# A second FFN in seven block products for two tiles, with row statistics taken in the attention

## The chip, the cores and the metric

The kernel runs on one core of a Trainium2 chip. Its time is device microseconds from one launch to its end. Five engines work beside each other, and each takes its own instructions in a fixed order: TensorE (PE in the profile; its weight loads are PEld), VectorE (DVE), ScalarE (ACT), GpSimd (POOL) and SyncE (SP). PE writes into PSUM banks, and DVE or ACT bring the results to SBUF. Semaphores tie the engines together.

## The reference

The input x has 2048 rows (tokens) of 1024 float32 numbers. The block is a macaron: half an FFN, an attention with a convolution, half an FFN.

```python
x = x + 0.5 * ffn(layernorm(x))
x = x + attn(layernorm(x))        # convolution of width 3, then causal attention in blocks of 128 tokens
x = x + 0.5 * ffn(layernorm(x))

def ffn(x):                       # the same weights in both
    routing = softmax(x @ gate_w.T)              # 8 experts
    in_scale = routing @ in_channel_scale
    out_scale = routing @ out_channel_scale
    return x * in_scale @ sign(weight).T * out_scale + bias
```

The change is in the second FFN and in the attention ahead of it.

## The kernel before

The first FFN runs to about 200 us, the convolution to about 420, the attention to about 780, and the second FFN to the end. The rows are worked on in 16 tiles of 128.

**The second FFN (class `Ffn`).** For one tile `sums_of` takes the row statistics (two `bn_stats`, their sum, an epsilon on DVE; a power and a shift on POOL) and ACT writes the normalized rows `xn`. `transpose` turns them on PE in two halves, and ACT copies the halves into `xnT`. `gate` multiplies with the gate's weights, `route` makes the softmax over 8 experts: the largest logit on DVE (`nm`), the exp on ACT, then the reciprocal and a high and a low part (`rhl`) on DVE. `turn` transposes these on PE (`rt`) and DVE copies them (`rT`). `scale` multiplies `rT` with the input scales on PE (`is`), DVE multiplies `xnT` by them, ACT casts each half to the fp32r format (the high term), and POOL subtracts for the low term, so that two passes of matmuls keep the accuracy. `out_scale` makes the output scales on PE (`po`), and ACT halves them into `os`. `main` runs 32 matmuls of 128x512: 8 chunks of the inner dimension, 2 terms, 2 halves of the columns. DVE multiplies each half by `os` and adds it into the row. `add_bias` adds half the bias to the row by a transfer that accumulates, issued from POOL. The signs of the weights stay in SBUF (`sw2`).

**What sets the order.** `run` writes out PE's order by hand: `main` of one tile, with the gate, route, transposes and turn of later tiles between its halves. On DVE, ACT and POOL a scheduler decides the order when the kernel is built, from the program's order and its own costs. Loads and stores go through SP's queue. The row buffers of the second FFN form a ring of nine (`load_rows2`): two shared with the sign loads (`aside`), three of their own, four of the attention's ring.

**The attention.** It runs over 4 groups g of 512 tokens, and for each group 4 turns r of two pairs of heads: queries and keys (`stage_qk`), scores, softmax, transposes, values and the output weights (`stage_wo`). In the second turn of the next group `stage_proj` projects the four tiles of a group and DVE adds them to the residual rows (L1116); SP stores them. In the same turn the signs of two chunks of the FFN's weights are loaded and taken on ACT. The last group's projection lies at the end, interleaved by hand with the start of the second FFN (tiles 0 to 2).

Of the kernel before, what the change touches and what calls it, by code (L numbers as in the profile page):

```python
# [17 lines left out]
P = 128  # L18
# [6 lines left out]
def kernel(  # L25
# [42 lines left out]
    const.tile([P, 80], F32, name="left_edge")  # L68
    sbq = const.tile([P, NHP], F32, name="sbq")
    spill = pool(ctx, "spill", 1, space=DRAM)  # L70
# [117 lines left out]
    class Ffn:  # L188
# [12 lines left out]

        def norm(self, t, pinned=False, on_vector=False):
            for n in range(t, min(t + 2, self.end)):
                self.ahead(n)
            self.norm_sums(t, pinned, on_vector)()
# [8 lines left out]
        def transpose(self, t, copies=(nc.scalar.copy, nc.scalar.copy)):  # L214
            xn = self.xns.pop(t)
            xnT = self.work.tile([P, DC, P], F32, name=f"xnT_{self.name}_{t}", tag="xnT", bufs=3)
            for h, copy in enumerate(copies):
                tr = bank("tr", [P, 4, P], f"tr_{self.name}_{t}_{h}")
                for c in range(4):
                    nc.tensor.transpose(tr[:, c, :], xn[:, ts(4 * h + c, P)], ident)  # L220
                copy(xnT[:, 4 * h : 4 * h + 4, :], tr)  # L221
            self.xnTs[t] = xnT
# [66 lines left out]
        def out_scale(self, t):  # L289
            rT = self.rTs.pop(t)  # L290
            osc = self.work.tile([P, D], F32, name=f"os_{self.name}_{t}", tag="osc")
            pos = [bank("acc", [P, NB], f"po_{self.name}_{t}_{h}") for h in range(NH2)]
            for h, po in enumerate(pos):
                rows = ts(NH2 + h, QC)
                nc.tensor.matmul(po, lhsT=rT[rows, :], rhs=tables[rows, :], start=True, stop=True)
            for h, po in enumerate(pos):
                nc.scalar.mul(osc[:, ts(h, NB)], po, 0.5)  # L297
            self.oscs[t] = osc
# [48 lines left out]
        def run(self, first):  # L347

            self.behind = first > self.first
            for t in range(first, self.end):
                if t + 2 not in self.lgps:
                    self.on(self.gate, t + 2)
                if t + 1 < self.end:
                    self.scale(t + 1, out=True)
                self.main(t, 0)
                self.on(self.route, t + 2)
                self.on(self.transpose, t + 3)
                self.on(self.between, t - 2)  # L360
                self.on(self.norm, t + 4, t < self.kept)
                self.on(self.add_bias, t + 4)
                self.main(t, 1, beside={DC - 2: lambda: self.on(self.turn, t + 2)})
                self.on(self.after, t - 1)
                self.beside(t)

# [571 lines left out]
    def leave(t, h):  # L938

        if t + 1 == NT:  # L940
            nc.sync.dma_start(out=out[ts(t, P), ts(h, NB)], in_=rows[t][:, ts(h, NB)])

    with ExitStack() as ph:
        ow = pool(ph, "ow", 1)
        ap4 = pool(ph, "ap4", 4)
        vhp = pool(ph, "vhp", 1)
        ap2 = pool(ph, "ap2", 2)
        qkt.append(pool(b2, "qkt1", 1, side="right"))
# [153 lines left out]

        def stage_proj(g, b, kinds=("mm", "tr")):
# [13 lines left out]
            t = g * BPG + b  # L1117
            x3[t] = spill.tile([P, D], F32, name=f"x3_{t}")
# [16 lines left out]

        def turn(g, r, values):
# [7 lines left out]
            if r == 1:  # L1144
                raws = [signs(2 * g + n) for n in range(2)]
# [20 lines left out]
        with tc.manual_schedule(engines={mybir.EngineType.PE}):  # L1166
            for i in range(LAST - 1):
                turn(*divmod(i, NP), True)
                if i == LAST - 3:
                    for t in range(2):  # L1170
                        load_rows2(t)
                if i == LAST - 2:
                    load_residual(NG - 1)
            g, r = pairs[-1]
            begun = {}
            xn_of = {}
            for t in range(2):
                with tc.issue_after(stored[g - 1].ins):
                    begun[t] = sums_of(
                        lambda t=t: xn_of[t], rows[t], f"f2_{t}", on_vector=t, later=True  # L1180
                    )
# [4 lines left out]
            work = pool(f2, "work2", 2, side="right")  # L1186
            xn2 = pool(f2, "xn2", 3, side="right")
            later.append(pool(f2, "rring2", 3, side="right"))
            ffn = Ffn("f2", sw2, work, xn2, 0, NT, lambda t: rows[t], load_rows2, store, lambda t: None, lambda t: None, NT, leave)
            two(stage_wo, LAST - 3)  # L1190
            two(stage_transpose, LAST - 2, "sm", "tr")
            for t in range(2):
                ffn.xns[t] = xn_of[t] = xn2.tile([P, D], F32, name=f"xn_f2_{t}", tag="xn")
                begun[t]()

            def begin_tile(t):
                ffn.norm(t, t > 0)
                ffn.add_bias(t)

# [12 lines left out]
            stage_transpose(g, NHP - 1, "mm")  # L1212
            stage_wo(g, NHP - 2)
# [4 lines left out]
            with tc.issue_after(ended[g].ins):  # L1218
                begin_tile(2)
            one = ("mm", "mm")  # L1220
            stage_proj(g, 0, one)
            ffn.turn(0)
            ffn.transpose(2)
            stage_proj(g, 1, one)
            ffn.scale(0, out=True)
            ffn.route(1)
            stage_proj(g, 2, one)
            stage_proj(g, 3, one)
            ffn.turn(1)
            begin_tile(3)  # L1230
    ffn.run(0)
# [55 lines left out]
```

## Time and profile before

| | |
|---|---|
| time, median of 3 runs | 940.31 us (939.81 to 940.38) |
| the profiled execution | 940.06 us, its span 938.3 us |
| busy: PE, PEld | 920.0 us (98%), 659.5 us (70%) |
| busy: DVE, ACT, POOL | 662.3 us (71%), 462.0 us (49%), 235.7 us (25%) |
| HBM traffic | 89.30 MB read, 37.85 MB written |
| bias into a row (POOL's queue) | 5.3 us from issue to landing |
| row load, row store (SP's queue) | 4.5 us, 2.6 us |

The span is the time from the first to the last instruction that the profiler recorded. Busy is the time in which an engine had an instruction at work; matmuls are pipelined and their ends are modelled, so the sum of the lengths of single matmuls is more than the busy time. In lines of the timeline, `x2` stands for two instructions in a row, and a bracket at the end tells how long the engine had been idle and what ended that.

### The profile page before, as it was taken

The page shows a single profiled execution, that of the slowest core. Times are in us where ns is not written, and L with a number is a line of the kernel's source. Part 1 is how long each engine was busy: PE and PEld are TensorE (multiplying, and loading weights), DVE is VectorE, ACT ScalarE, POOL GpSimd, SP SyncE. Part 2 cuts the span into 40 slices and gives each one's busy share as a digit, 9 for nine tenths or more (in the row PEclk, how much of TensorE's full clock was granted, in tenths as well). Part 3 has the DMA queues.
Part 4 walks back from the last instruction along what each step waited for, and adds up shares of the span by engine and source line. Part 5 has one row for each costly group of instructions (what it writes and reads, how often), then busy time and mean ns, then how long its engine had stood idle before and what let it go on. Part 6 is the DMA issues. An engine that isn't in the chain of part 4 may idle for free.

```text
span 938.3 us, 14525 instructions
## 1 busy us (share of the span) xinstructions
PE 920.0 (98%) x5240; PEld 659.5 (70%) x5240; DVE 662.3 (71%) x1326; ACT 462.0 (49%) x1258; POOL 235.7 (25%) x330
## 2 busy tenths in 40 slices
PE   6999999999999999999999999999999999999998
PEld 4678878886666666675876577567765756788786
DVE  5888887789978677656686557656746666666654
ACT  5676666431111111126886567666855844454441
POOL 2554453220011100101231113013201404444341
PEclk9999999999999999999999999999999999999999
DMA  9776653499567765536360245032406737655341
GB/s 343 181 199 192 178 182 136 186 274 353 181 201 195 190 188 135 117 108 222 116 135 23 75 154 133 23 140 89 88 1 209 150 114 210 172 163 152 90 114 67
DMA packets 39543, 144.86 MB, mean 154 GB/s; under 512 B 5096, under 2 KB 6120, under 8 KB 37552
## 3 DMA queue, kind: packets, MB, share of 16 engines
q1 hardware_dynamic: 28048, 97.91, 28.9%
q0 software_dynamic: 10688, 38.02, 20.9%
q10 hardware_dynamic: 736, 8.02, 2.3%
q8 instruction: 41, 0.67, 0.3%
q14 instruction: 30, 0.25, 0.1%
HBM read 89.30 MB, written 37.85 MB: 136 GB/s over the span
## 4 chain that ended last, share of the span: by engine, by line
PE 80%; DVE 7%; ACT 6%; DMA 3%; issue 3%; POOL 1%; POOLq 0%; DVEq 0%; ACTq 0%
PE cv L544 23%; PE pm_f L311 19%; PE pq L829 7%; PE pp L1108 6%; PE pv L829 5%; PE acc L1084 4%; PE sc L1012 3%; PE tr_f L220 3%; PE pt L1054 2%; DMA x<-in_x_dram 2%; ACT p L1039 2%; PE ao L1067 2%; PE lgp_f L228 2%; PE is_f L272 1%; ACT qk L972 1%
## 5 line engine op out<-in xcount | busy, mean ns | idle before, releaser
L311 PE MATMUL pm_f<-sw,y_f 128*128 128x512 f32 x1024 | 258.4, 403 | 0.6 <-ACT y_f L285 0.4
L311 PEld LDWEIGHTS pm_f<-sw,y_f 128*128 128x128 f32 x1024 | 186.8, 190 | 41.9 <-ACT y_f L285 0.8
L544 PE MATMUL cv<-v,u 128*128 128x342 f32 x576 | 166.0, 450 | 0.0
L544 PEld LDWEIGHTS cv<-v,u 128*128 128x128 f32 x576 | 109.2, 190 | 56.7
L1025 POOL TENSOR_SCALAR_AFFINE_SELECT p<-p 128x512 f32<-128x512 f32 x64 | 38.5, 635 | 249.6 <-ACT p L1021 249.6
L1039 ACT ACTIVATE p<-p,anm 128x128 f32<-128x128 f32 x256 | 99.8, 396 | 0.0
L561 ACT ACTIVATE m<-cv 128x342 f32<-128x342 f32 x42 | 19.2, 456 | 154.4 <-PE cv L544 152.3
L323 DVE TENSOR_TENSOR pm_f<-pm_f,os_f 128x512 f32<-128x512 f32 x64 | 44.6, 697 | 68.6 <-PE pm_f L311 68.5
L286 POOL TENSOR_TENSOR y_f<-xnT_f,y_f 128x512 fp32r<-128x512 f32 x63 | 80.0, 1288 | 45.3 <-ACT y_f L285 45.3
L1035 DVE TENSOR_REDUCE anm<-p 128x4 f32<-128x512 f32 x64 | 39.6, 678 | 26.9 <-POOL p L1025 26.9
L1084 PE MATMUL acc<-oT,wo_sb 128*128 128x512 f32 x128 | 58.0, 595 | 0.2 <-DVE oT L1076 0.2
L544 PE MATMUL cv<-v,g 128*128 128x342 f32 (+2 forms) x224 | 57.1, 415 | 0.8 <-DVE v L466 0.8
L1108 PE MATMUL pp<-pw_sb,o2T 128*128 128x512 f32 x128 | 56.4, 596 | 0.0
L221 ACT COPY xnT_f<-tr_f 128x512 f32<-128x512 f32 x58 | 33.6, 588 | 41.6 <-PE tr_f L220 39.9
L544 PEld LDWEIGHTS cv<-v,g 128*128 128x128 f32 x224 | 39.7, 190 | 17.6 <-DVE v L466 1.2
L1039 ACT ACTIVATION_READ_ACCUMULATOR p<-p,anm 128x1 f32 x256 | 49.9, 195 | 0.0
L1059 DVE COPY pT<-pt 128x512 f32<-128x512 f32 x32 | 22.1, 690 | 38.8 <-PE pt L1054 38.8
L972 ACT ACTIVATE qk<-pq,sbq 128x256 f32<-128x256 f32 x64 | 30.0, 469 | 39.5 <-PE pq L829 39.5
L1047 DVE TENSOR_TENSOR p<-p,asum 128x512 f32<-128x512 f32 x64 | 45.1, 704 | 1.3
L1108 PEld LDWEIGHTS pp<-pw_sb,o2T 128*128 128x128 f32 x128 | 23.7, 190 | 29.1 <-issue 26.1
L297 ACT ACTIVATE os_f<-po_f 128x512 f32<-128x512 f32 x64 | 34.8, 595 | 16.8 <-PE is_f L272 6.7
L285 ACT CAST y_f<-xnT_f 128x512 fp32r<-128x512 f32 x64 | 37.6, 626 | 11.1 <-DVE xnT_f L283 11.1
(186 smaller groups left out, 1668.0 us busy)
## 6 DMA issues: line engine op xcount, KB each, us to landing
g<-in_conv_w_dram SPq DMA_DIRECT2D x28, 512.0 KB, 5.2
u<-in_conv_w_dram POOLq DMA_DIRECT2D x24, 512.0 KB, 6.1
x<-in_x_dram SPq DMA_DIRECT2D x16, 512.0 KB, 5.5
raw<-in_weight_t_dram SPq DMA_DIRECT2D x16, 512.0 KB, 6.5
x<-hbias POOLq DMA_DIRECT2D x16, 512.0 KB, 5.3
x<-x SPq DMA_DIRECT2D x16, 512.0 KB, 4.1
xr<-x SPq DMA_DIRECT2D x16, 512.0 KB, 4.9
xr<-in_proj_b_dram POOLq DMA_DIRECT2D x16, 512.0 KB, 9.1
```

Source lines behind the costliest of these rows:

```text
L286: lows[h].tensor_tensor(yl, y, yh.bitcast(F32), ALU.subtract)
L311: ins = nc.tensor.matmul(pms[h], lhsT=y[:, n, c, :], rhs=self.sw[:, c, ts(h, NB)], start=(c == 0 and n == 0), stop=(c == DC - 1 and n == 1),)
L323: nc.vector.tensor_tensor(pms[h], pms[h], o, ALU.mult)
L544: nc.tensor.matmul(accs[w, k][:, lo:hi], lhsT=uk[:, c, :], rhs=V[k][:, c, lo:hi], start=(c == 0), stop=(c == DC - 1),)
L829: nc.tensor.matmul(leave.sums[sums], lhsT=rows[a][:, u, :], rhs=cols[b], start=n in (0, 1, 3), stop=True, skip_group_check=True,)
L972: nc.scalar.activation(h, acc, AF.Identity, bias=bias, scale=(QSCALE, 1.0)[n])
L1025: nc.gpsimd.affine_select(out=p, in_=p, pattern=[[0, BPG], [-1, P]], compare_op=ALU.is_ge, fill=NEG_INF, base=0, channel_multiplier=1,)
L1035: nc.vector.tensor_reduce(nmax, p, AX.X, ALU.max, negate=True)
L1039: exps[g, r] = nc.scalar.activation(p[:, b, :], p[:, b, :], AF.Exp, bias=nmax[:, b : b + 1], accum_out=asum[:, b : b + 1],)
L1047: nc.vector.tensor_tensor(p, p, asum.unsqueeze(2).broadcast_to([P, BPG, P]), ALU.mult)
L1084: nc.tensor.matmul(accs[g][m], lhsT=wo_sb[:, hp, ts(m, P)], rhs=oT, start=(hp == 0), stop=(hp == NHP - 1),)
L1108: nc.tensor.matmul(pp, lhsT=o2T[:, m, ts(b, P)], rhs=pw_sb[:, m, ts(h, NB)], start=(m == 0), stop=(m == WC - 1),)
```

## The change

The second FFN takes two tiles at a time. With the tiles as rows and halves of the inner dimension as columns, a pair's scaled input is four blocks a11, a12, a21, a22, the signs are four blocks b11 to b22, and the output is four blocks. A form of Strassen's and Winograd's multiplication makes the output from seven products (the class's `PRODUCTS`) in place of eight. It needs four sums of input blocks (s1 to s4, on DVE; s1 takes the place of a21), four sums of sign blocks (t1 to t4), and sums of products, which partly accumulate in PSUM and partly are added on DVE from copies that ACT makes. The new class `Pairs` writes out the order of a pair (`period`).

- The low terms of all seven blocks are made on DVE, not on POOL.
- The row statistics of tiles 0 to 11 are taken in the attention, in `stage_proj`, as soon as their rows are complete, and kept in small tiles. Tiles 12 to 15 keep theirs in the second FFN.
- The output goes to a tile of its own (`to`), and a transfer that accumulates, on POOL's queue, adds it to the row, for tiles 0 to 13. The last pair is added on DVE and stored by halves.
- The signs are loaded 2, 3 and 3 chunks in the first three groups, where it was 2 in each of the four, and the 16 sums of sign blocks are made on DVE in the last turns of the attention and beside the last projection.
- At the start, tiles 0 to 3 are normalized, transposed and gated, and tiles 0 and 1 scaled, before the first main product.
- There are more buffers: `xnT` has four, the high and low terms eight of half size, the output scales four.

```diff
     sbq = const.tile([P, NHP], F32, name="sbq")
+    means, rstds, shifts = (
+        [const.tile([P, BPG, n], F32, name=f"{name}_{g}") for g in range(NG - 1)]
+        for name, n in (("means", 2), ("rstds", 1), ("shifts", 1))
+    )
     spill = pool(ctx, "spill", 1, space=DRAM)
...
-        def out_scale(self, t):
+        def out_scale(self, t, kind="acc", pl=None):
             rT = self.rTs.pop(t)
-            osc = self.work.tile([P, D], F32, name=f"os_{self.name}_{t}", tag="osc")
-            pos = [bank("acc", [P, NB], f"po_{self.name}_{t}_{h}") for h in range(NH2)]
+            osc = (pl or self.work).tile([P, D], F32, name=f"os_{self.name}_{t}", tag="osc")
...
+    class Pairs(Ffn):
+        depth = 4
+        PRODUCTS = (("a11", "b11"), ("a12", "b21"), ("s2", "t2"), ("s1", "t1"), ("s3", "t3"), ("s4", "b22"), ("a22", "t4"))
...
+        def scale_in(self, t, kind):
+            xnT, rT = self.xnTs[t], self.rTs[t]
+            scs = [bank(kind, [P, 4, P], f"is_{self.name}_{t}_{h}") for h in range(NH2)]
...
+            for h, sc in enumerate(scs):
+                y = xnT[:, 4 * h : 4 * h + 4, :]
+                nc.vector.tensor_tensor(y, y, sc, ALU.mult)
+        def block_sums(self, p):
+            (a11, a12), (a21, a22) = (
+                [self.xnTs[t][:, 4 * h : 4 * h + 4, :] for h in range(2)] for t in (2 * p, 2 * p + 1)
+            )
+            s2, s3, s4 = (self.sp.tile([P, 4, P], F32, name=f"{n}_{p}", tag=n) for n in ("s2", "s3", "s4"))
+            sub = nc.vector.tensor_tensor
+            sub(s3, a11, a21, ALU.subtract)
+            sub(a21, a21, a22, ALU.add)
+            sub(s2, a21, a11, ALU.subtract)
+            sub(s4, a12, s2, ALU.subtract)
+            self.blocks[p] = {"a11": a11, "a12": a12, "s1": a21, "a22": a22, "s2": s2, "s3": s3, "s4": s4}
+        def split(self, p, *names):
+            for n in names:
+                a = self.blocks[p][n]
+                y = self.halves[p, n] = self.yp.tile([P, 2, 4, P], F32R, name=f"y_{self.name}_{p}_{n}", tag="y")
+                nc.scalar.copy(y[:, 0], a)
+                nc.vector.tensor_tensor(y[:, 1], a, y[:, 0].bitcast(F32), ALU.subtract)
+            if "a22" in names:
+                for t in (2 * p, 2 * p + 1):
+                    del self.xnTs[t]
+        def product(self, p, n):
...
+            acc = self.sums_of_pair[p][(0, 1, 0, 1, 0, 1, 0)[n]]
+            a, b = self.PRODUCTS[n]
+            y = self.halves.pop((p, a))
+            for c in range(4):
+                for part in range(2):
+                    nc.tensor.matmul(
+                        acc,
+                        lhsT=y[:, part, c, :],
+                        rhs=self.cols[b][c],
+                        start=(n in (0, 1, 3) and c == 0 and part == 0),
+                        stop=(c == 3 and part == 1),
+                        skip_group_check=True,
+                    )
+            i, h, first, last = {
+                0: (0, 0, True, False),
+                1: (0, 0, False, True),
+                2: (0, 1, True, False),
+                3: (1, 1, True, False),
+                4: (1, 1, False, True),
+                5: (0, 1, False, True),
+                6: (1, 0, True, True),
+            }[n]
+            t = 2 * p + i
+            if t not in self.outs:
+                self.outs[t] = self.tp.tile([P, D], F32, name=f"to_{t}", tag="to")
+            o, osc = self.outs[t][:, ts(h, NB)], self.oscs[t][:, ts(h, NB)] if last else None
+            if first and last:
+                nc.vector.tensor_tensor(o, acc, osc, ALU.mult)
+            elif first:
+                nc.scalar.copy(o, acc)
+            else:
+                nc.vector.tensor_tensor(o, acc, o, ALU.add)
+                nc.vector.tensor_tensor(o, o, osc, ALU.mult)
+            if not last:
+                return
+            if t + 2 >= self.end:
+                xt = self.row(t)[:, ts(h, NB)]
+                nc.vector.tensor_tensor(xt, xt, o, ALU.add)
+                self.leave(t, h)
+            elif n > 4:
+                nc.gpsimd.dma_start(out=self.row(t), in_=self.outs[t], accum_op=ALU.add)
+                self.store(t)
+        def period(self, p):
+            c, d, e, f, g, h = (2 * p + k for k in range(2, 8))
+            more = d < self.end
+            self.product(p, 0)
+            for t in (g, h):
+                self.on(self.ahead, t)
+            for t in (c, d):
+                self.on(self.turn, t)
+            self.product(p, 1)
+            if more:
+                self.scale_in(c, "tr")
+                self.scale_in(d, "acc")
+                self.block_sums(p + 1)
+                self.split(p + 1, "a11", "a12")
+            self.product(p, 2)
+            self.on(self.transpose, e)
+            if more:
+                self.split(p + 1, "s2", "s1")
+            self.product(p, 3)
+            self.on(self.transpose, f)
+            self.on(self.begin_tile, g)
+            if more:
+                self.split(p + 1, "s3")
+            self.product(p, 4)
+            for t in (e, f):
+                self.on(self.gate, t)
+            if more:
+                self.out_scale(c, "acc", self.op)
+                self.out_scale(d, "tr", self.op)
+                self.split(p + 1, "s4")
+            self.product(p, 5)
+            for t in (e, f):
+                self.on(self.route, t)
+            self.on(self.begin_tile, h)
+            if more:
+                self.split(p + 1, "a22")
+            self.product(p, 6)
...
+        def row_statistics(g, b):
+            mv, rs = means[g][:, b, :], rstds[g][:, b, :]
+            stats = small.tile([P, NH2, 6], F32, name=f"st_f2_{g}_{b}", tag="stats")
+            for h in range(NH2):
+                nc.vector.bn_stats(out=stats[:, h, :], in_=rows[g * BPG + b][:, ts(h, NB)])
+            nc.vector.bn_aggr(out=mv, in_=stats)
+            nc.vector.tensor_scalar(rs, mv[:, 1:2], EPS, None, ALU.add)
+            nc.gpsimd.tensor_tensor(rs, rs, nhalf, ALU.pow)
+            nc.gpsimd.tensor_scalar(shifts[g][:, b, :], mv[:, 0:1], rs, -1.0, ALU.mult, ALU.mult)
         def stage_proj(g, b, kinds=("mm", "tr")):
...
             t = g * BPG + b
+            if g + 1 < NG:
+                row_statistics(g, b)
...
+        SIGNS = (range(2), range(2, 5), range(5, 8), ())
...
-                raws = [signs(2 * g + n) for n in range(2)]
+                raws = [signs(c) for c in SIGNS[g]]
...
+                if i == LAST - 4:
+                    first = [
+                        vt.tile([P, WC, HE], F32R, name="t3", tag="wv_sb"),
+                        vt.tile([P, 3, NB], F32R, name="t2", tag="wv_sums"),
+                        vt.tile([P, 3, HT], F32R, name="t2_last", tag="vs"),
+                        vt.tile([P, WC, NB], F32R, name="t4", tag="vx"),
+                    ]
+                    b11, b12, b21, b22 = (
+                        [sw2[:, 4 * j + c, ts(h, NB)] for c in range(4)] for j in range(2) for h in range(NH2)
+                    )
+                    t3 = [first[0][:, c // 2, ts(c % 2, NB)] for c in range(4)]
+                    t2 = [first[1][:, c, :] for c in range(3)] + [first[2].rearrange("p n e -> p (n e)")[:, 0:NB]]
+                    t4 = [first[3][:, c, :] for c in range(2)]
+                    cols = {"b11": b11, "b21": b21, "t2": t2, "t1": b12, "t3": t3, "b22": b22, "t4": t4}
+                    def sign_sums(*names):
...
+                            for o, x0, x1 in zip(out_, in0, in1):
+                                nc.vector.tensor_tensor(o, x0.bitcast(F32), x1.bitcast(F32), ALU.subtract)
                 if i == LAST - 3:
+                    sign_sums("t3", "t1")
                     for t in range(2):
                         load_rows2(t)
                 if i == LAST - 2:
+                    sign_sums("t2")
                     load_residual(NG - 1)
             g, r = pairs[-1]
-            begun = {}
-            xn_of = {}
-            for t in range(2):
-                with tc.issue_after(stored[g - 1].ins):
-                    begun[t] = sums_of(
-                        lambda t=t: xn_of[t], rows[t], f"f2_{t}", on_vector=t, later=True
-                    )
             stage_qk(g, r)
...
+            def normalize2(t):
+                load_rows2(t)
+                g, b = divmod(t, BPG)
+                if g + 1 == NG:
+                    ffn.norm_sums(t)()
+                    return
+                xn = ffn.xns[t] = xn2.tile([P, D], F32, name=f"xn_f2_{t}", tag="xn")
+                if t == 1:
+                    nc.vector.tensor_scalar(xn, rows[t], means[g][:, b, 0:1], rstds[g][:, b, :], ALU.subtract, ALU.mult)
+                else:
+                    nc.scalar.activation(xn, rows[t], AF.Identity, bias=shifts[g][:, b, :], scale=rstds[g][:, b, :])
+            def begin_tile(t):
+                normalize2(t)
+                ffn.add_bias(t)
+            ffn.begin_tile = begin_tile
...
             stage_values(g, NHP - 2)
             stage_transpose(g, NHP - 1, "mm")
+            begin_tile(2)
             stage_wo(g, NHP - 2)
             stage_values(g, NHP - 1)
             ffn.route(0)
             ffn.gate(1, "tr")
             stage_wo(g, NHP - 1)
             with tc.issue_after(ended[g].ins):
-                begin_tile(2)
+                begin_tile(3)
+            inner.close()
+            ys = pool(f2, "ys", 8, side="right")
+            sp = pool(f2, "sp", 1, side="right")
+            tp = pool(f2, "tp", 3, side="right")
+            ffn.begin(cols, store, ys, sp, tp)
             one = ("mm", "mm")
+            ffn.transpose(2)
             stage_proj(g, 0, one)
             ffn.turn(0)
-            ffn.transpose(2)
+            ffn.route(1)
             stage_proj(g, 1, one)
-            ffn.scale(0, out=True)
-            ffn.route(1)
+            ffn.scale_in(0, "tr")
+            ffn.turn(1)
+            ffn.transpose(3)
+            sign_sums("t4")
             stage_proj(g, 2, one)
+            ffn.scale_in(1, "acc")
+            ffn.block_sums(0)
+            ffn.gate(2)
+            ffn.gate(3)
+            ffn.split(0, "a11", "a12", "s2")
             stage_proj(g, 3, one)
-            ffn.turn(1)
-            begin_tile(3)
-    ffn.run(0)
+            ffn.split(0, "s1", "s3", "s4", "a22")
+            ffn.route(2)
+            ffn.route(3)
+    with tc.manual_schedule(engines={mybir.EngineType.PE}):
+        ffn.op = pool(f2, "osc2", 4, side="right")
+        ffn.out_scale(0, "acc", ffn.op)
+        ffn.out_scale(1, "tr", ffn.op)
+        ffn.begin_tile(4)
+        ffn.begin_tile(5)
+        for p in range(NT // 2):
+            ffn.period(p)
```

## The prediction

> **What bounds the kernel now.** I read the page's totals first, then the second FFN by windows of one pair of tiles, its chain in order of time, and its timeline.
>
> ```profile
> PE 920.0 (98%) x5240; PEld 659.5 (70%) x5240; DVE 662.3 (71%) x1326; ACT 462.0 (49%) x1258; POOL 235.7 (25%) x330
> ...
> PEclk9999999999999999999999999999999999999999
> ...
> PE 80%; DVE 7%; ACT 6%; DMA 3%; issue 3%; POOL 1%; POOLq 0%; DVEq 0%; ACTq 0%
> ```
>
> TensorE is busy 98% of the span at a full granted clock. The window below is one pair of tiles (columns: window, its length, then busy time of PE, PEld, DVE, ACT, POOL, the clock, the DMA share, GB/s).
>
> ```profile
> 801.88:821.64 19.76, 19.76 (x140) 15.88 (x139) 13.07 (x31) 9.48 (x21) 8.50 (x10) 1.00 0.56 161
> ```
>
> PE fills the pair's 19.76 us and DVE uses 13.07. The chain in order of time says the same: a tile is PE work laid end to end, 9.88 us, with no other engine in it.
>
> ```profile
> 811.76 3.86 PE pm_f L311 x16
> 815.62 0.12 PE lg_f L241 x2
> 815.74 0.93 PE tr_f L220 x8
> 816.67 2.77 PE pm_f L311 x12
> 819.44 0.11 PE rt_f L260
> 819.55 0.93 PE pm_f L311 x4
> ```
>
> So fewer matmuls pay only while the other engines keep up. Their paces stand in the timeline (start, us, engine, line).
>
> ```profile
> 811.97 1.28 DVE L283 TENSOR_TENSOR xnT_f<-xnT_f,is_f 128x512 f32<-128x512 f32 x2
> 812.05 1.09 ACT L297 ACTIVATE os_f<-po_f 128x512 f32<-128x512 f32 x2
> ...
> 815.66 0.70 DVE L323 TENSOR_TENSOR pm_f<-pm_f,os_f 128x512 f32<-128x512 f32 x1 [2.41 <-PE pm_f L311]
> ...
> 816.39 0.69 DVE L324 TENSOR_TENSOR xf<-xf,pm_f 128x512 f32<-128x512 f32 x1
> ...
> 816.80 0.27 ACT L246 ACTIVATE ro_f<-lg_f,nm_f 128x8 f32<-128x8 f32 x1
> ...
> 817.20 0.16 DVE L248 RECIPROCAL rsum_f<-rsum_f 128x1 f32<-128x1 f32 x1
> ```
>
> Two independent DVE operations take 1.28, each 0.68 long, so the second starts 0.60 after the first. The add L324 needs the product L323 and starts 0.73 after it. ACT's L297 pair gives 0.49 a step, and the casts L285 (1.15 for two) 0.52. Exp to reciprocal, ACT to DVE, is 0.40. The tail shows the hand-overs and PE alone:
>
> ```profile
> 919.80 1.28 DVE L283 TENSOR_TENSOR xnT_f<-xnT_f,is_f 128x512 f32<-128x512 f32 x2
> ...
> 920.57 1.17 ACT L285 CAST y_f<-xnT_f 128x512 fp32r<-128x512 f32 x2 [0.23 <-DVE xnT_f L283]
> 921.27 2.55 POOL L286 TENSOR_TENSOR y_f<-xnT_f,y_f 128x512 fp32r<-128x512 f32 x2 [6.40 <-ACT y_f L285]
> ...
> 930.23 0.70 DVE L323 TENSOR_TENSOR pm_f<-pm_f,os_f 128x512 f32<-128x512 f32 x1 [2.28 <-PE pm_f L311]
> ...
> 933.86 0.70 DVE L323 TENSOR_TENSOR pm_f<-pm_f,os_f 128x512 f32<-128x512 f32 x1 [2.21 <-PE pm_f L311]
> ```
>
> DVE to the cast that needs it: 0.77. Cast to the low term: 0.70. Sixteen matmuls: 933.86 - 930.23 = 3.63, so 0.228 each and 1.83 for a product of eight. From the last matmul's end to DVE: 0.31 (sixteen from 811.69 end at 815.35, L323 starts at 815.66).
>
> **The change, part by part.** PE: 64 main matmuls a pair become 56: 8 x 0.228 = 1.82 less. The other PE work stays: 1.08 + 0.11 + 0.80 + 0.59 = 2.58 a tile from the chain (logits and transposes, rt, gate, scales). PE alone would need 56 x 0.228 + 5.16 = 17.9 a pair, 14.6 less over eight pairs.
>
> DVE: a pair had 12 operations of 128x512 (4 input scalings, 4 products, 4 adds) and 4 row statistics. It now has 4 scalings, 4 block sums, 7 low terms, 3 adds and 4 products: 22 x 0.60 plus dependences and some 2.5 of small routing work, nearly 16 of the period. That alone would fit into 17.9. What decides is the order: an engine takes its instructions in turn, and the built order of the changed kernel, read engine by engine, closes a loop from product 1 (a12) of one pair to product 1 of the next.
> - Product 1 runs 1.83, then 0.31: the add of products 0 and 1 starts 2.14 after it.
> - On DVE behind that add: product with the out scale 0.73, scaling 0.60, scaling 0.60; low term of a11, which waits for ACT's cast of a11 (0.77 + 0.70 after its scaling), 0.84; two scalings, s3, low a12 and s1, five steps of 0.60; s1 to s2 0.73; s2 to its cast 0.77. Sum 7.27.
> - ACT then runs without a gap: casts s2, s1 (1.04), copy of product 3 (0.49), two transpose copies (0.97), casts s3, s4 (1.04), logits copy (0.14 to the next, 811.91 to 812.05), one norm (1.15), logits copy (0.14), four out scales (1.96), cast a22 (0.52), and only then the first exp. Sum 7.45.
> - Exp to reciprocal 0.40. Then DVE: 0.16, max of the other tile 0.13, routing 0.25, low a22 0.60, routing 0.25, reciprocal 0.16, product with the out scale of product 6 0.60, routing 0.29, and 0.36 to the transpose rt. Sum 2.80.
> - rt 0.14, and PE may begin the next product 1.
>
> 2.14 + 7.27 + 7.45 + 0.40 + 2.80 + 0.14 = 20.2 a pair, against 19.76 before and 17.9 of PE's own. PE waits some 2.3 in each pair (at the second rt, and at the second gate, for ACT's copies) where it waited for nothing. The matmul saving is spent waiting on the loop.
>
> Between the starts of product 1 I take 20.2 three times. Tiles 12 to 15 still get their statistics on DVE (two of 0.60 to 0.68 a tile, some ahead of s2): 21.5 and 20.9. Then 19.9, where no norm is left on ACT but the cast of a22 waits for product 5. The next interval has no transposes and gates: 16.6, with PE's own 14.0 (12.8 of products, 2 x 0.59 of scales) as its lower bound. From the last product 1 to PE's end 6 x 1.83 = 11.0.
>
> The start: main matmuls began at 780.75. Now the transposes, gates and scalings of tiles 1 to 3 come first, and product 0 begins at about 785.4; then rt of tile 3 waits, because the exps of tiles 2 and 3 stand on ACT behind five casts and four out scales: product 1 at about 790.4. PE's end: 790.4 + 60.6 + 21.5 + 20.9 + 19.9 + 16.6 + 11.0 = 940.9. Before, it was 918.95 + 14.6 = 933.6. That is +7.3. The tail (4.7 from there to the span's end) keeps its product, add and half-row store. The three dependent steps before it (2.06) exceed the product (1.83): +0.2.
>
> Attention: the statistics of tiles 0 to 11 put 1.2 + 0.4 on DVE for each tile, 6.4 per group, into the projection stage, where DVE idles 1.02 before each of the L1116 adds; POOL's pow and shift (0.56 + 0.26) lie in front of selects (L1025) that wait for ACT anyway. Sixteen sign sums of 0.60 lie before the copies pT and queue in front of the qk adds for 0.2 to 0.35. The third sign load of a group waits for a row of the ring, with ACT idle. In the last group 3.3 of statistics go away. Together 0 to +3; I take +0.5, as the rows with idle DVE are the nearest.
>
> The residual: 14 accumulating transfers go to POOL's queue, and each store on SP waits for one. Nearest row: the bias transfer, 0.9 to issue and 5.3 to landing; with store 2.6 and next load 4.5 it is 13.3, while a row of the ring has about 30 between the end of its pair and its next use: hidden, 0. If that cover failed, the norm would be late by the excess, pair by pair. It takes three DVE adds a pair away, already counted.
>
> The low terms free POOL (four of 1.28 a pair) and load DVE with seven of 0.60, also counted; two of them lie in the loop.
>
> Sum: the profiled execution took 940.06, a span of 938.3 and 1.76 around it, 0.25 under the median. Span 938.3 + 7.3 + 0.2 + 0.5 = 946.3; with 1.76, 948.1. Forecast **948**.
>
> A rule that speaks against the change is weighed here. The row says 0.60 from one DVE start to the next. The Trainium skill, "VectorE: DVE Perf Modes", section "The DRAIN you can't avoid", says that the next operation does not start until the pipeline is empty. By it each of the loop's nine independent DVE steps would take its full 0.68, the loop 20.9 and the time about 952; the row shows a start before that, so 0.60 stands in the sum.
>
> **The rivals.** *PE stays the bound (faster).* The loop may be shorter than I add up, if ACT gets to the exps earlier or hand-overs overlap. For it: DVE, ACT and POOL each have idle time in every pair, and the chain before names only PE. Against it: the order is fixed. With the loop at or under 17.9: 790.4 + 6 x 17.9 + 14.0 + 11.0 = 922.8 instead of 933.6, plus 0.7 and 1.76 on the span, makes 930. It takes 2.3 less of waiting in each pair; at 18.9 (8.0 over six intervals) the two kernels are equal.
>
> *DVE steps at full price (slower still).* Many of the new steps wait on another engine, and the row of a step that waits is 0.73 (L323 to L324), not 0.60. Nine steps at 0.13 more make the loop 21.4, six intervals 7.0 more: 955.
>
> *A row comes late from the ring.* If accumulating, storing and loading took 30 instead of 13.3, each norm would be late: a microsecond over is six in all, so two over make 960. The DMA share of 0.56 in the window speaks against it.
>
> *The change does not do what it says.* The built order has 448 main matmuls for 512, the statistics in the attention and no low term of this FFN on POOL; excluded.
>
> **How the numbers follow.** Forecast (944 to 952 as its own range) 0.57; PE stays the bound, 928 to 937, 0.20; full price, 952 to 959, 0.15; the ring or a dearer attention 0.06; equal, 0.02. A measurement of this kernel tells 0.2%, 1.9 us, from no change. Faster 0.21, same 0.03, slower 0.76. The range leaves out the lower part of the PE rival and the ring: 934 to 958.
>
> **What would show it.** In the changed profile: PE's share below 98% in the second FFN, with waits of rt on DVE's routing and of the gate on ACT's copies; about 20.2 between products 1; DVE idle some 1.6 before the first add of a pair; exp behind four out scales on ACT; the first main matmul near 785; the attention within a microsecond. Windows of 18 with PE full would make the forecast wrong, and so would an SP store or a norm that waits for a transfer.

## The result, and the profile after

| | before | after |
|---|---|---|
| time, median | 940.35 us (939.81 to 940.86, 4 runs) | 953.74 us (953.54 to 955.66, 4 runs) |
| span of the profiled execution | 938.3 us | 951.6 us |
| first main matmul of the second FFN | 780.75 us | 787.05 us |
| its last main matmul's end | 933.6 us | 946.6 us |

The ratio is 1.0147, with an interval of 1.013 to 1.0165: the change costs 13.4 us, where 7.7 were forecast. The time lies in the wide range of the prediction (934 to 958) and above the forecast's own range of 944 to 952.

The page of the kernel after, the same three rows as before:

```profile
PE 919.1 (97%) x5176; PEld 653.5 (69%) x5176; DVE 715.4 (75%) x1426; ACT 487.9 (51%) x1306; POOL 209.8 (22%) x313
...
PEclk9999999999999999999999999999999999998999
...
PE 69%; DVE 11%; ACT 9%; DMA 6%; issue 3%; POOL 1%; POOLq 0%; DVEq 0%; ACTq 0%
```

TensorE does 64 matmuls less (5176 for 5240), but it is busy for only 0.9 us less (part of that time at half its clock, see pair 3 below), and its share of the chain falls from 80% to 69%: VectorE, ScalarE and transfers stand there now. The clock has a dent near the end.

Little of it arises before the second FFN, and none where the change adds work to the attention. The projection of group 0 begins 1.52 us later than before (528.70 for 527.18) and that of group 2 1.45 later (705.90 for 704.45), so nothing is lost between them, with the statistics and sign loads in place. Of the 1.5, 0.66 is there when the convolution begins, and the rest arises at 425 to 435 us, in the attention's first softmax, where the change moves nothing by its text.

The last row of the table is the start of the last product (944.72) and eight matmuls of 0.228. From product 1 of a pair to that of the next, by the starts in PE's timeline (the last by the middle of sixteen matmuls in a row), in us:

| pair | 0 | 1 | 2 | 3 | 4 | 5 | 6 |
|---|---|---|---|---|---|---|---|
| forecast | 20.2 | 20.2 | 20.2 | 21.5 | 20.9 | 19.9 | 16.6 |
| measured | 19.72 | 19.78 | 21.69 | 25.55 | 21.44 | 19.22 | 16.4 |

**A pair without late rows.** The chain in order of time of the kernel after (start, us, what), in pair 1; the lines left out are of the same kind:

```profile
811.74 1.84 PE pm_f L439 x8
...
813.68 0.70 DVE to L465
814.38 0.02 issue
814.40 0.69 DVE to L466
...
820.11 0.70 DVE s L415
...
824.64 1.15 ACT xn_f L1385
825.78 0.15 ACT lgs_f L242
825.93 1.96 ACT os_f L303 x4
827.89 0.51 ACT y_f_a L423
828.40 0.27 ACT ro_f L252 x2
...
830.80 0.29 DVE rhl_f L259
831.09 0.14 issue
831.23 0.30 PE rt_f L266
```

This is the loop of the prediction, in its order: product, add, scalings and block sums on VectorE, casts and copies, norm and four out scales on ScalarE, the exp (L252), the routing, the transpose. From product 1 to the add it is 2.18 (2.14 had been taken), to the cast of s2 at 820.84 7.16 (7.27), to the exp 7.56 (7.45), and from there to rt 2.83 (0.40 + 2.80). The window of that pair:

```profile
811.50:831.28 19.78, 19.00 (x131) 14.55 (x132) 15.68 (x32) 12.60 (x27) 3.44 (x5) 1.00 0.83 213
```

PE is busy 19.00 of 19.78 us. It lacks only 0.8, not the 2.3 of the forecast, because its own work is not 17.9.

**Pair 3, which the prediction had not seen.** The chain again, from the end of pair 2:

```profile
852.58 6.18 DMA xf<-to
858.76 0.02 issue
858.77 2.92 DMA out_dram<-xf
861.70 0.02 issue
861.71 6.57 DMA xf<-x
868.28 0.02 issue
868.30 0.07 DVE st_f L171
```

An accumulating transfer adds the output of tile 5 to its row, the store follows, then the load of tile 14 into the same buffer, then VectorE's statistics of that tile: 15.7 us in a row. Tile 13 takes tile 4's buffer in the same way, from 850.76 on. The timeline shows what stands behind it:

```profile
864.24 0.69 DVE L171 BATCH_NORM_STATS2 st_f<-xf 128x6 f32<-128x512 f32 x1 [2.71 <-DMA xf<-x]
864.85 0.68 DVE L415 TENSOR_TENSOR s<-xnT_f,xnT_f 128x512 f32<-128x512 f32 x1
...
867.72 0.97 PE L234 MATMUL lgp_f<-xnT_f,gate_sb 128*32 128x128 f32 x16 [3.60 <-ACT xnT_f L227]
...
869.77 3.78 PE L439 MATMUL pm_f<-sw,y_f_s 128*128 128x512 f32 x8
```

VectorE stands 2.71 us for the row of tile 13, and s2 (L415) is behind it in its order. In pair 2 it had stood 2.44 us in the same way for the row of tile 12, at 843.76. ScalarE's casts and copies come late, the gate waits 3.60, and then a product takes 3.78 us instead of 2.1. The windows around it give the granted clock in the third column from the end:

```profile
865.00:869.00 4.00, 1.22 (x18) 0.70 (x20) 3.74 (x9) 3.44 (x7) 0.00 (x0) 0.93 0.68 170
869.00:873.00 4.00, 4.00 (x12) 2.67 (x11) 3.42 (x8) 2.43 (x6) 2.19 (x3) 0.50 0.01 4
```

After the idle window TensorE ran at half its clock; that product took some 1.7 us more, and one at 892 us, in pair 4, some 1.6 more (3.66). Little of this is added to the pair, by an estimate from the timeline: the norm of tile 13, late by its statistics, runs on ScalarE at 870.93, and with the out scales behind it the exp comes only at 874.65. In pair 1 the next product 1 followed 2.88 after the exp, here 3.87 (878.52), so a full clock would have given back at most 1.0 here and, by the same count, 0.3 in pair 4. The Trainium skill, "TensorE: Matmul & The Clock Gate", section "What's actually happening", puts the drop to half rate after an idle window of about 3.4 us; the wait of 3.60 fits, while the longest single wait ahead of the second drop was 0.98.

### The profile page after: what moved, and what is told of

It reads as the page before. It is cut to its first block, busy times and chain, and to the rows that moved or that the text cites. A ratio compares the mean times of both kernels' runs of the same rounds, so it can differ in the third digit from the quotient of the medians.

```text
span 951.6 us, 14534 instructions
## 1 busy us (share of the span) xinstructions
PE 919.1 (97%) x5176; PEld 653.5 (69%) x5176; DVE 715.4 (75%) x1426; ACT 487.9 (51%) x1306; POOL 209.8 (22%) x313
## 4 chain that ended last, share of the span: by engine, by line
PE 69%; DVE 11%; ACT 9%; DMA 6%; issue 3%; POOL 1%; POOLq 0%; DVEq 0%; ACTq 0%
PE cv L692 23%; PE pm_f L317 8%; PE pq L977 8%; PE pp L1265 5%; PE pv L977 5%; PE acc L1231 4%; PE sc L1159 3%; PE pm_f L439 3%; PE pt L1201 3%; PE ao L1214 2%; DMA x<-in_x_dram 2%; ACT p L1186 2%; PE tr_f L226 2%; DVE xnT_f L405 1%; DMA xf<-to 1%
## 5 line engine op out<-in xcount | busy, mean ns | idle before, releaser
L317 PE MATMUL pm_f<-sw,y_f 128*128 128x512 f32 x512 | 132.6, 409 | 0.6 <-ACT y_f L291 0.4
L317 PEld LDWEIGHTS pm_f<-sw,y_f 128*128 128x128 f32 x512 | 94.5, 193 | 22.0 <-ACT y_f L291 0.8
L709 ACT ACTIVATE m<-cv 128x342 f32<-128x342 f32 x42 | 19.2, 456 | 153.5 <-PE cv L692 151.4
L292 POOL TENSOR_TENSOR y_f<-xnT_f,y_f 128x512 fp32r<-128x512 f32 x31 | 39.4, 1282 | 20.2 <-ACT y_f L291 20.2
L680 DVE SCALAR_TENSOR_TENSOR u<-g,u 128x1024 f32<-128x1024 f32 x18 | 22.0, 1225 | 27.7 <-issue 11.0
L1168 ACT COPY p<-sc 128x512 f32<-128x512 f32 x64 | 32.9, 600 | 16.0 <-PE sc L1159 16.0
L1231 PEld LDWEIGHTS acc<-oT,wo_sb 128*128 128x128 f32 x128 | 24.1, 190 | 23.9 <-issue 22.2
```

The lines of the kernel that those rows point to most:

```text
L292: lows[h].tensor_tensor(yl, y, yh.bitcast(F32), ALU.subtract)
L317: ins = nc.tensor.matmul(pms[h], lhsT=y[:, n, c, :], rhs=self.sw[:, c, ts(h, NB)], start=(c == 0 and n == 0), stop=(c == DC - 1 and n == 1),)
L1168: copied = pin(nc.scalar.copy(p, acc)).ins
L1231: nc.tensor.matmul(accs[g][m], lhsT=wo_sb[:, hp, ts(m, P)], rhs=oT, start=(hp == 0), stop=(hp == NHP - 1),)
```

## The experiments

The theory: the loop of 19.75 us a pair, and late rows for the tiles whose statistics stay on VectorE, make the loss. Rivals: the accumulating transfers by themselves; ScalarE's place in the loop is slack; TensorE and VectorE set the pace; the start is VectorE's.

**Statistics of tiles 12 to 15 borrowed.**

```diff
-                g, b = divmod(t, BPG)
-                if g + 1 == NG:
-                    ffn.norm_sums(t)()
-                    return
+                g, b = min(t // BPG, NG - 2), t % BPG
```

> Leaves out the row statistics of tiles 12 to 15 (they are normalized with those of tiles 8 to 11), so nothing on VectorE waits for their rows and only ScalarE's norms read them. Theory A (the built order closes a loop of 19.75 us a pair, and the statistics left on VectorE ask for rows 13 to 15 some 12 us after the pair that frees their buffers, so VectorE stands and the block sums behind them are late): the intervals between products 1 of 21.7, 25.6 and 21.4 us fall to 19.8 each, 9.3 less in all, time about 944.5. Theory B (the accumulating transfers make the rows late for whoever reads them, the norm on ScalarE too): only the VectorE work of the statistics goes, about 1.9 + 1.3 + 0.7, time about 950.

Measured: 944.47 us (944.02 to 944.85), ratio 1.0044 (1.0029 to 1.0059). The intervals are 19.72, 19.80, 19.80, 19.79, 19.81, 19.21. Theory A held. So 9.3 us of the 13.4 are the statistics that stayed and what waited for their rows, the slow clock included (here it does not fall). The transfers are all still there: with nobody on VectorE asking early, they cost nothing that shows. The 4.0 us that remain lie ahead of the pairs: product 0 begins at 786.84 where the kernel before began its main matmuls at 780.75, with work of tiles 1 to 3 moved ahead of it, and from there to the span's end it takes 155.3 us instead of 157.6.

**Out scales behind the routing.**

```diff
-            if more:
-                self.out_scale(c, "acc", self.op)
-                self.out_scale(d, "tr", self.op)
                 self.split(p + 1, "s4")
             self.product(p, 5)
             for t in (e, f):
                 self.on(self.route, t)
+            if more:
+                self.out_scale(c, "acc", self.op)
+                self.out_scale(d, "tr", self.op)
```

> Only the order of a pair is changed: the out scales of the next pair come after the routing, so the exps stand behind one or two of the four on ScalarE. Theory A: the exp starts some 1.3 us earlier (it then waits for product 5 and the largest logit), and a pair without late rows takes about 18.4 us instead of 19.75; the pairs that wait for rows gain little. Three to four such intervals: about 949. Rival (the loop is TensorE's and VectorE's own, ScalarE's place in it is slack): within 1 us of 953.7.

Measured: 954.69 us (953.9 to 956.63). The first two intervals are 19.31 and 19.39, 0.4 shorter, not 1.3. The exp does come 1.1 earlier after product 1 (15.84 for 16.90), but a second loop lies just under the first: s2's cast, the copies of the transposes, the second gate, and from there TensorE's own work without a gap (the gate waited 0.35 in this pair). VectorE stood longer for the rows (6.5 us in all instead of 5.4), in intervals of 22.41 and 27.52 instead of 21.69 and 25.55. So the time lies within the rival's 1 us by chance, two effects against each other, and neither account held: ScalarE's place matters, but only to the next limit.

**Low terms on GpSimd.**

```diff
-                nc.vector.tensor_tensor(y[:, 1], a, y[:, 0].bitcast(F32), ALU.subtract)
+                nc.gpsimd.tensor_tensor(y[:, 1], a, y[:, 0].bitcast(F32), ALU.subtract)
```

> The seven low terms of a pair go from VectorE to GpSimd (1.28 us each there, 9 a pair). Theory A: the loop loses 0.84 + 0.60 and 0.60 of VectorE steps and becomes about 17.9 to 18.4 us, TensorE's own need; the accumulating transfers queue behind low terms on GpSimd, so rows 13 to 15 are as late or 1 to 2 us later. Time about 947, 944 to 950. Rival (GpSimd's queue becomes the bound, with the transfers and the low terms one behind the other): 953 or more.

Measured: 962.17 us, ratio 1.0231 (1.0214 to 1.0248); intervals 22.79, 21.84, 21.86, then 25.96 and 24.89. The timeline of this run has low terms on POOL beside VectorE's work:

```profile
841.69 2.98 POOL L424 TENSOR_TENSOR y_f_a<-xnT_f,y_f_a 128x512 fp32r<-128x512 f32 x2 [4.76 <-ACT y_f_a L423]
842.59 0.93 DVE L413 TENSOR_TENSOR s<-xnT_f,xnT_f 128x512 f32<-128x512 f32 x1
843.56 1.66 DVE L414 TENSOR_TENSOR xnT_f<-xnT_f 128x512 f32<-128x512 f32 x1
...
855.18 1.57 DVE L258 TENSOR_SCALAR rhl_f<-ro_f,rsum_f 128x64 fp32r<-128x64 f32 x1
```

L414 takes 1.66 where it took 0.69, L258 1.57 where it took 0.25: the steps that VectorE was spared come back as longer ones. The Trainium skill, "SBUF — State Buffer", section "Who interferes with whom", has VectorE's second input from SBUF go through a port shared with GpSimd, and one of the two wait for the whole instruction; the length of L414, which has two such inputs, agrees with that. For L258, with one tile and a number per row as inputs, the cause was not tried. The time is in the rival's range, but not by its cause: GpSimd is busy 13.13 of 21.84 us, and the chain of that pair has none of its work. In the chain a norm stands ahead of the copies of the transposes here. A lower clock is not needed: it was 0.92 in the pair of 21.84, but 1.00 in the one of 21.86. In the latter the second gate comes 12.58 after product 1 (11.50 in pair 1 of the change) and the next product 1 9.28 after the gate (8.28), so about half of the 2.1 us arises on each side of it; how the norm and the longer steps share them was not tried.

**The residual on VectorE.**

```diff
-            if t + 2 >= self.end:
-                xt = self.row(t)[:, ts(h, NB)]
-                nc.vector.tensor_tensor(xt, xt, o, ALU.add)
-                self.leave(t, h)
-            elif n > 4:
-                nc.gpsimd.dma_start(out=self.row(t), in_=self.outs[t], accum_op=ALU.add)
-                self.store(t)
+            xt = self.row(t)[:, ts(h, NB)]
+            nc.vector.tensor_tensor(xt, xt, o, ALU.add)
+            if t + 2 >= self.end:
+                self.leave(t, h)
+            elif n > 4:
+                self.store(t)
```

> The output is added to the row on VectorE and stored (four adds of 0.60 to 0.73 more a pair), no accumulating transfer. Theory A: rows are free some 6 us earlier, so rows 13 to 15 are there in time and the interval of 25.6 falls to about 22; against that one or two adds enter the loop, 0.6 to 1.3 a pair. Time 952 to 957. Theory B (the transfers are the main cause): about 946.

Measured: 953.95 us (953.45 to 955.25), as the change itself and as theory A had it (theory B: about 946). The intervals are 22.15, 20.65, 20.64, 21.16, 21.95 and 20.41. The one of 25.55 falls to 21.16, VectorE standing for no row, and the plain ones rise to 20.65: two of the four adds stand in the loop. The first is 1.5 longer still, since its product 1 took 3.66 us at a granted clock of 0.67 (792 to 796 us). So the two totals agree by chance.

**All statistics at the projection.** `row_statistics` also for the last group; nothing on VectorE in the second FFN.

```diff
-            if g + 1 < NG:
-                row_statistics(g, b)
+            row_statistics(g, b)
```

> All 16 tiles' statistics are taken at their projection, those of tiles 12 to 15 too; nothing is left out. Theory A (the late rows cost what the borrowed statistics saved): intervals of 19.8 us as there, and four times 1.6 us of VectorE in the start, where VectorE has 13 of 40 us idle: 0 to +3 on 944.5, so 944.5 to 947. Rival (the start is VectorE's, every step in it counts): 950 or more.

Measured: 950.93 us (949.92 to 951.42). The intervals are 20.87, four of 19.83 to 19.84, and 19.32, but the first product 1 starts at 796.45, 4.7 later than with the change. The rival was right: PE's waits in the start hold 4.2 us for the routing and this one:

```profile
776.91 1.31 PE L226 MATMUL tr_f<-ident,xn_f 128*128 128x128 f32 x8 [1.54 <-DVE rstds L1256]
```

VectorE's idle time there is not free, since it lies in between steps that TensorE waits for. The waits are not all of it: the clock fell twice, behind this wait (0.77 in 780 to 784 us, eight matmuls of the projection 5.29 us instead of 3.60) and behind the wait of 4.2 (0.64 in 796 to 800, product 1 3.22 instead of 2.07). By the starts these two stretches make some 2.8 of the 6.5 us over the run with borrowed statistics.

**TensorE alone.** Borrowed statistics, late out scales, and no low terms.

```diff
-                nc.vector.tensor_tensor(y[:, 1], a, y[:, 0].bitcast(F32), ALU.subtract)
...
-                        lhsT=y[:, part, c, :],
+                        lhsT=y[:, 0, c, :],
```

> Leaves out: the low terms (TensorE multiplies the high terms twice, the same 56 matmuls a pair) and the statistics of tiles 12 to 15; out scales after the routing. VectorE loses seven steps of 0.60 a pair, so the loop is at most 17.7 us and the interval between products 1 is TensorE's own need. The forecast had that need at 17.9 a pair: time about 935. The traces since show TensorE busy 19.0 of the 19.8 with two waits of 0.35 left: then the interval is about 19.0 and the time about 940 to 941.

Measured: 937.72 us (937.19 to 938.33), ratio 0.9973 (0.9963 to 0.9983); intervals 19.25, 19.27, 19.23, 19.24, 19.24. With VectorE at 11 us a pair:

```profile
830.10:848.70 18.60, 18.34 (x126) 14.17 (x125) 11.19 (x25) 12.70 (x26) 3.45 (x4) 1.00 0.85 219
```

So a pair costs 19.2 even where only TensorE is short of time (it waits 0.2 for the gate). The time is 2.3 us below the 940 to 941 expected, though the pair is longer than the 19.0 expected: the start is shorter, with product 1 at 788.31 instead of 791.78. From start to start in pair 2 of this run, the seven products take 13.63 and the rest 5.60.

**The best put together**: all statistics at the projection and late out scales, as in the diffs above, and at the start the exps of tiles 2 and 3 ahead of the out scales.

```diff
             stage_proj(g, 3, one)
-            ffn.split(0, "s1", "s3", "s4", "a22")
             ffn.route(2)
             ffn.route(3)
+            ffn.split(0, "s1", "s3", "s4", "a22")
...
-            for h, po in enumerate(pos):
-                nc.scalar.mul(osc[:, ts(h, NB)], po, 0.5)
+            with tc.issue_after(after.ins) if after else ExitStack():
+                for h, po in enumerate(pos):
+                    nc.scalar.mul(osc[:, ts(h, NB)], po, 0.5)
```

> All statistics at the projection, out scales after the routing in each pair, and at the start the exps of tiles 2 and 3 ahead of the first out scales on ScalarE. Nothing is left out. Theory A: 944.5 to 947, less 5 x 0.45 for the second loop (through the gate) that takes over at 19.35, less about 2 at the start, where TensorE waits 2.1 for the routing of tile 3: 940.5 to 943. Rival (another wait at the start takes its place): 943 to 945.

Measured: 946.26 us (945.68 to 947.92), ratio 1.0068 (1.0053 to 1.0083). The first interval is 20.90, the others 19.42 to 19.48, but the start keeps its cost: product 1 at 792.92, with 2.7 us of waiting for the routing and 1.5 for the statistics left. The 1.4 us more in the first interval are product 1, which took 3.52 us at a clock of 0.58 (792 to 796 us). The expectation missed by 3, and the rival by 1: the start, as in the run with all statistics at the projection, and the clock.

**Parts alone, in the kernel before.** First the statistics of tiles 0 to 11 at their projection, with `row_statistics` as in the change:

```diff
             t = g * BPG + b
+            if g + 1 < NG:
+                row_statistics(g, b)
...
+            ffn.norm = norm2
```

(`norm2` normalizes with them, as `normalize2` does in the change.)

> The kernel before with one part of the change alone: the row statistics of tiles 0 to 11 at their projection. Theory A: no cost, as TensorE sets the time there and in the second FFN: 940.4, within 1 us. Rival (the statistics delay the adds of the projection and the stores behind them): 942 to 944.

Measured: 939.19 us (939.03 to 940.19, 10 runs) against 940.56, ratio 0.9988 (0.9979 to 0.9998): no cost, and possibly 1 us of gain, within what was called no change. Then the low terms on VectorE as well:

```diff
-        def scale(self, t, copy=nc.scalar.copy, out=False, lows=(nc.gpsimd, nc.gpsimd)):
+        def scale(self, t, copy=nc.scalar.copy, out=False, lows=(nc.vector, nc.vector)):
```

> The kernel before with two parts of the change alone: the statistics of tiles 0 to 11 at their projection and the low terms on VectorE (both FFNs), without the products of pairs. Theory A: TensorE sets the time and has the work of before; VectorE's load in a pair goes from 13.1 to about 12.8, so 939 to 940, no more than 0.5 from the statistics alone. Rival (low terms between VectorE's products hold the scalings up): 942 or more.

Measured: 945.15 us (944.89 to 948.24), ratio 1.0053 (1.0041 to 1.0066). The time is in the rival's range, but not by its cause in the second FFN: the edit also reaches the first FFN, and the loss arises there and on the way: the last group's projection begins at 768.82 instead of 764.09. From there to the span's end it takes 174.1 against 173.6. So on VectorE the low terms cost 0.5 in the second FFN of before; the rest belongs to a place that the change leaves alone.

**Statistics behind the routing.** Both norms of a pair, and the statistics of tiles 12 to 15, come after the routing in the order; late out scales and the start's order as in the best above.

```diff
-            self.on(self.begin_tile, g)
...
             if more:
-                self.out_scale(c, "acc", self.op)
-                self.out_scale(d, "tr", self.op)
                 self.split(p + 1, "s4")
...
+            if more:
+                self.out_scale(c, "acc", self.op)
+                self.out_scale(d, "tr", self.op)
+                self.split(p + 1, "a22")
+            self.on(self.begin_tile, g)
             self.on(self.begin_tile, h)
-            if more:
-                self.split(p + 1, "a22")
...
-                    ffn.norm_sums(t)()
+                    with tc.issue_after(ffn.routed.ins):
+                        ffn.norm_sums(t)()
```

> Nothing is left out. In each pair both norms and, for tiles 12 to 15, their statistics come behind the routing, so VectorE asks for rows 13 to 15 some 8 us later and the block sums don't stand behind them; the out scales come behind the routing too, and at the start the exps stand ahead of the out scales. Theory A (the rows were late only for VectorE's early place in the order): no wait of more than 1 us for a transfer, intervals of about 19.3, two or three of them 1.5 longer for the statistics, 2 less at the start: 941 to 944. Theory B (the rows are late whenever they are read): one interval stays over 23, 946 or more.

Measured: 941.79 us (941.11 to 943.16, 10 runs), ratio 1.0014 (1.0004 to 1.0023). Intervals 19.39, 19.38, 19.37, 19.31, 20.21, 20.19: no pair waits for a row, though the transfers are still there, so theory A held. VectorE asks for tile 13's row at some 868 us, 23 us after the transfer into the buffer's former row was issued (844.95), where it was 10.8 in the change. The clock did not fall. TensorE's two largest waits in the whole second FFN, as sum, number and longest:

```profile
PE lgp_f L234 <- ACT xnT_f L227: 3.5, 6, 1.1
PE pm_f L440 <- DVE to L466: 1.3, 1, 1.3
```

It is 12 us faster than the change, and still no faster than before.

## Why the prediction was right in its direction and short in its size

- **The loop** was right, link by link: 19.75 against 20.2. Two sizes were off by 0.1 and made up for each other, and the last stretch, from the exp to the transpose, was 2.83 for 3.20; the 0.31 from TensorE's end to VectorE rested on an end (815.35) that was worked out from 0.228 a matmul, not read, and yet the add came 2.18 after product 1 for 2.14; the independent steps on VectorE do start 0.60 apart (two scalings, L405, take 1.28).
- **The full-price rival** (955) came closest by its number and is wrong by its cause: with steps of 0.73 the plain pairs would take 21.4, and they took 19.75. The same goes for the rule of the pipeline that must empty first.
- **The ring** is the step that failed. It was priced at 13.3 us of transfers under a cover of 30, so 0; a norm that waits for a transfer had been named as a sign against the forecast, and it was the statistics ahead of the norm that waited. The transfers took 15.7 in the chain (6.18 to accumulate, 6.57 to load), and the cover of 30 was counted to the norm on ScalarE. For tiles 12 to 15 the first reader is the statistics on VectorE, in the order ahead of s2: in pair 3 it asked for tile 13's row at 861.53, 10.8 after the transfer into the buffer's former row was issued, and the row came after 13.5. The forecast charged 1.3 and 0.7 for the instructions of the statistics and missed the wait. This, with the clock behind it, is 4.05 in pair 3; pair 2 was 1.5 over (statistics of tile 12 and the wait for its row, for which nothing had been charged) and pair 4 0.5. Against these 6.1 the other intervals were 1.8 shorter than forecast and product 1 began 1.4 later, together the 5.7 that the forecast fell short by. The borrowed statistics gave back 9.3, of which 2.0 were in the sum. The rival of a late row from the ring (960) had this cause, with transfers of more than 30 us in place of an early reader.
- **TensorE's own need** was 19.0 to 19.2, not 17.9, a mistake that the loop hid. The prediction had the saving of the matmuls spent by waiting on the loop; most of it was never there. The 0.228 of a matmul was read in the tail, where 64 run in a row. Between other work it is 13.63 / 56 = 0.243, and it was that before, too: pieces of 3.77, 2.86 and 1.11 for 32 matmuls. The small work was 2 x 2.14 = 4.28 a pair before by these starts and is 5.4 to 5.6 now: one place for scales and out scales (0.59 a tile) became two (0.52 and 0.33), and the gates went from 0.57 to about 0.75 a tile. Of the eight matmuls saved, 1.9 us, some 0.5 to 0.75 stay. So the rival in which PE stays the bound would not have been at 930: the run without low terms is at 937.7.
- **The start** was right: product 0 at 787.05 for 785.4, product 1 at 791.78 for 790.4, with the 1.45 that was there before the second FFN. What was taken as attention (0.5) was 0 by the change's parts and 1.45 by the traces; that the order at 425 us is another chance of the scheduler was only argued.
- **The tail** was right: 5.0 from PE's end to the span's end, with 4.7 + 0.2 forecast.

## What to carry to other kernels

Before a saving of matmuls is counted, read a pair's price start to start where the matmuls stand between other work, and count what splitting the small work costs: here it ate two thirds of the saving. When a buffer ring gets one more link, look for the first reader in the order of every engine, not for the main one; here a statistic placed early stopped an engine for a row that its norm read 9 us later. And in a loop over several engines a shortened link pays only down to the next loop, which here lay 0.4 below.

## What the runs showed of the hardware

- TensorE's granted clock fell to 0.50 after a wait of 3.60 us, and the product behind it took 1.7 us more. A second drop (0.57 in 892 to 896 us) came where the longest single wait was 0.98. After waits of 2.1 and 0.2 us ahead of the first product 1 it stayed at 1.00 in the change and fell to 0.67 in the run with the residual on VectorE.
- An addition of two SBUF tiles on VectorE took 1.66 us beside a subtraction on GpSimd, against 0.69 in the change, where GpSimd has no such work, and a small scaling 1.57 against 0.25.
- The accumulating transfer from SBUF to SBUF took 4.6 to 6.2 us in the chains, as long as the bias transfer from the page (5.3).
